# Softmax sums from a column of ones, weights turned first, and gates taken by ScalarE, in a two-part transformer kernel

## The chip, the cores and the metric

The kernel runs on one core of a Trainium2 chip. Time is device time in microseconds (us) of one launch of the whole program. An engine's instructions run in the order in which they were issued to it; the engines run beside each other and wait for each other through semaphores. TensorE (PE) multiplies matrices and turns tiles, VectorE (DVE), ScalarE (ACT) and GpSimd (POOL) work element by element, SyncE (SP) issues the transfers (DMAs). TensorE writes to PSUM alone[...]; GpSimd does not touch it.

## The reference, cut to what matters

The input has 8 sequences of 512 tokens and 128 channels, in float32. A first part normalises it and adds an attention of 16 heads with another weighting than the softmax; the change does not touch it. The second part runs six layers, each an attention over a window and a gated feed-forward:

```python
def local_attention(q, k, v):            # 16 heads of 64, windows of 32 tokens
    ...
    bk2, bv2 = (look(bk), look(bv))      # each window with the one before it: 64 keys
    ...
    sim = jnp.einsum('bhwie,bhwje->bhwij', bq, bk2) * QK_SCALE
    sim = jnp.where(mask, -jnp.finfo(sim.dtype).max, sim)
    attn = jax.nn.softmax(sim, -1)
    out = jnp.einsum('bhwij,bhwje->bhwie', attn, bv2)

def ffn_layer(x, g, bln, W1, b1, W2, b2):
    ...
    hg = xn @ W1 + b1
    a, gate = jnp.split(hg, 2, -1)       # 341 columns each
    return a * jax.nn.gelu(gate, approximate=False) @ W2 + b2

for i in range(DEPTH):                   # 6
    x = attn_layer(shift_tokens(x), Wqkv[i], q_scale[i], k_scale[i], Wo[i]) + x
    x = ffn_layer(shift_tokens(x), ln_g[i], ln_b[i], W1[i], b1[i], W2[i], b2[i]) + x
```

Ahead of the scores q and k are divided by their norms, scaled and rotated.

## The kernel before

The second part goes through layers, in a layer through the 8 sequences, in a sequence through two halves of 8 heads: 96 halves. A half is four pairs of heads, so there are 384 pairs, and the loop at the end takes one step t for each. A pair passes through several steps, so that one step works on several pairs at once. In a step, in the order of the text:

- `turn` (pair t): TensorE turns q and k, 8 transposes (L619), ScalarE copies them out (L624).
- `share` (pair t-2): VectorE sums the exponentials of a row (L662) and takes the reciprocal (L665) into `rs`, which the next step reads.
- `gather` (pair t-3): TensorE multiplies the turned weights with v, 32 small products of 64 keys by 32 queries by 64 columns, two instructions each (L685); VectorE multiplies what comes out with `rs` (L693).
- `turn_weights` (pair t-2): TensorE turns the exponentials (L673), ScalarE copies them out (L674).
- `prepare_qk`, for a quarter of the tokens of the next half: q and k of 8 heads (L552); ScalarE squares them (L557), VectorE sums the squares (L558) and multiplies with the rotary tables (L560, L568 twice), for q and then for k; GpSimd adds and scales (L572, L580); the norms go over L575 (VectorE), L576 and L577 (ScalarE).
- `exponentials` (pair t-1): ScalarE, L657. The text pins it behind all that stands ahead of it on ScalarE.
- `turn_sums` (pair t-3): TensorE turns the sums (L701), ScalarE copies them (L705).
- `weigh` (pair t): 32 small products for the scores (L639), VectorE adds the mask (L644) and takes the maxima (L649), GpSimd subtracts them (L650).
- `prepare_v`: v for a quarter of the tokens (L588), which ScalarE copies into `v` (L592). After the fourth quarter `spread` issues 18 DMAs on SP's queue (L604 to L609) that lay v out as `v3`, each window's keys on the partitions; `v3` is there twice, `v` once.
- one stage of a feed-forward, if one is under way, and then `leave` (pair t-3): the product with the output's weights (L711).

A feed-forward takes its stages in successive steps and comes once in 8 steps: turn the tokens (L733), normalise (L739 to L746), turn back (L753), the gates (L761 on TensorE; L764, VectorE, adds the bias and brings them from PSUM to `gate`), the other columns (L771, L774), and the product back to 128 channels (L782, L785). The gelu (L722) is done on ScalarE in the step after the gates, with a load of its table ahead of it and of the usual one behind it. By the step number modulo 8, its place, the stages stand so: L733 in place 4, L739 to L746 in 5, L753 in 6, L761 in 7, L771 in 0, L782 in 1; places 2 and 3 have none.

PSUM: five banks go round for the products and transposes of TensorE (tag "mm"), one buffer of two banks (tag "two") serves the scores and the sums of v in turn, one bank is the accumulator. So L685 has to wait until L644 has read the scores of the step before, and L639 until L693 has read the sums.

Order: the text is written through a library whose planner lays down each engine's order. It goes by the order of the text, with times of its own for each instruction, and lets a later instruction pass one whose operands or buffer are, by these times, not there yet. In the trace ScalarE's copies of v (L592) stand up to three steps behind their place in the text, and VectorE's L764 between L644 and L649. In all steps of the second part TensorE's order is that of the text.

Of the kernel before, what the change touches and what calls it, by code (L numbers as in the profile page):

```python
# [9 lines left out]
F32 = mybir.dt.float32  # L10
BF16 = mybir.dt.bfloat16
AF = mybir.ActivationFunctionType
ALU = mybir.AluOpType
AX = mybir.AxisListType
PSUM = bass.MemoryType.PSUM

P = 128
N = 512
NT = N // P
# [10 lines left out]
DHL = 64  # L30
INNER = H * DHL
NPAIR = H // 2
WIN = 32
QB = 32
KB = QB + WIN
NQ = N // QB
UB = P // QB
HH = H // 2
HC = HH * DHL
# [7 lines left out]
NCH = len(CH)  # L47
# [3 lines left out]
def tile_kernel(  # L51
# [18 lines left out]
    nc = tc.nc  # L70
# [38 lines left out]
    with ExitStack() as c1:  # L109
# [69 lines left out]
        xs = []  # L179
# [211 lines left out]
        for w in range(len(work) + 1):  # L391
            before, now, nxt = now, nxt, []
            if w + 1 < len(work):
                b, rbs = work[w + 1]
# [27 lines left out]
    k2 = ctx.enter_context(tc.tile_pool(name="k2", bufs=1))  # L422
    wp = ctx.enter_context(tc.tile_pool(name="wp", bufs=1))
    ep = ctx.enter_context(tc.tile_pool(name="ep", bufs=2))
    qp = ctx.enter_context(tc.tile_pool(name="qp", bufs=2))
    vp = ctx.enter_context(tc.tile_pool(name="vp", bufs=2))
    wo_p = ctx.enter_context(tc.tile_pool(name="wo_p", bufs=1))
    wf = ctx.enter_context(tc.tile_pool(name="wf", bufs=2))
    tp = ctx.enter_context(tc.tile_pool(name="tp", bufs=2))
# [4 lines left out]
    gate = wo_p.tile([P, NCH, N], F32, name="gate")  # L434
# [39 lines left out]
    rows = ep.tile([DEPTH, NV, P], F32, name="rows", tag="v", bufs=1)  # L474
# [8 lines left out]
    vec = k2.tile([P, NV, DEPTH], F32, name="vec")  # L483
# [45 lines left out]
    def shifted(b, name):  # L529
# [5 lines left out]
        nc.gpsimd.tensor_copy(xs[hf:D, 1:N], xT[hf:D, b, 0 : N - 1])  # L535
        return xs

    def begin(l, b, hv, xs):

        qn = [qp.tile([P, NT, HH, DHL], F32, name=f"qn{t}") for t in range(2)]  # L540
        v = ep.tile([P, NT, HC], F32, name="v", bufs=1)
        v3 = vp.tile([P, NQ, HC // 2], F32, name="v3")
        return dict(l=l, b=b, hv=hv, xs=xs, qn=qn, v=v, v3=v3)

    def prepare_qk(g, wqkv, tab, c):

# [35 lines left out]
            )  # L582

    def prepare_v(g, wqkv, c):
        xs, v = g["xs"], g["v"]
        lhsT = xs[:, c * P : (c + 1) * P]
        pv = ps_a.tile([P, HC], F32, name="pv2", tag="mm")
        nc.tensor.matmul(  # L588
            pv, lhsT=lhsT, rhs=wqkv[:, 2, :],
            start=True, stop=True,  # L590
        )
        nc.scalar.copy(v[:, c, :], pv)  # L592

    def spread(g):


        v, v3 = g["v"], g["v3"]
        for e in range(2):
            at = slice(e * KB, e * KB + WIN)
            cols = slice(e * (HC // 2), (e + 1) * (HC // 2))  # L600
            for u in range(UB):
                own = v[u * QB : (u + 1) * QB, :, cols]
                c = 1 if u == 0 else 0
                nc.sync.dma_start(v3[e * KB + WIN : (e + 1) * KB, u + c * UB :: UB, :], own[:, c:])  # L604
                if u < UB - 1:
                    nc.sync.dma_start(v3[at, u + 1 :: UB, :], own)
                else:
                    nc.sync.dma_start(v3[at, UB::UB, :], own[:, 0 : NT - 1])
            nc.sync.dma_start(v3[e * KB : (e + 1) * KB, 0, :], v[0:KB, 0, cols])  # L609


    def turn(a):
# [43 lines left out]

        tc.keep_in_program_order(nc.scalar.activation(flat, flat, AF.Exp))  # L657

    def share(a):

        a["rs"] = rs = tp.tile([P, 2 * NT], F32, name="rs", bufs=3)
        nc.vector.tensor_reduce(  # L662
            rs, a["pr"].rearrange("p c e k -> p (c e) k"), axis=AX.X, op=ALU.add
        )
        nc.vector.reciprocal(rs, rs)  # L665

    def turn_weights(a):

        pr = a["pr"]
        a["prT"] = prT = tp.tile([P, NT, P], F32, name="prT")  # L670
        pT = ps_a.tile([P, NT, P], F32, name="pT2", tag="mm")
        for c in range(NT):
            nc.tensor.transpose(pT[:, c, :], pr[:, c].rearrange("p e k -> p (e k)"), ident)  # L673
        nc.scalar.copy(prT, pT)  # L674

    def gather(a):

        g, p, prT = a["g"], a["p"], a["prT"]
        po = ps_b.tile([P, 2, N], F32, name="po2", tag="two")
        po = po[:, :, 0 : NT * DHL].rearrange("p e (c f) -> p e c f", c=NT)  # L680
        for n in range(NQ):
            c, u = n // UB, n % UB
            for e in range(2):
                rows = slice(e * KB, (e + 1) * KB)
                nc.tensor.matmul(  # L685
                    po[u * QB : (u + 1) * QB, e, c, :],
                    lhsT=prT[rows, c, u * QB : (u + 1) * QB],
                    rhs=g["v3"][rows, n, p * DHL : (p + 1) * DHL],
                    start=True, stop=True,
                )  # L690
        a["o"] = o = tp.tile([P, NT, 2, DHL], F32, name="o2")
        by = a["rs"].rearrange("p (c e) -> p e c", e=2).unsqueeze(3)
        nc.vector.tensor_tensor(  # L693
            o.rearrange("p c e f -> p e c f"), po, by.to_broadcast([P, 2, NT, DHL]), ALU.mult
        )

    def turn_sums(a):
# [28 lines left out]
    def feed_forward(b, l, w1, w2):  # L726

        xs = shifted(b, "xf")
        yield

        px = ps_a.tile([P, NT, D], F32, name="px", tag="mm")
        for c in range(NT):
            nc.tensor.transpose(px[:, c, :], xs[:, c * P : (c + 1) * P], ident)  # L733
        xt = tp.tile([P, NT, D], F32, name="xt", bufs=1)
        nc.scalar.copy(xt, px)
        st = tp.tile([P, NT, 6], F32, name="st")
        mv = tp.tile([P, NT, 2], F32, name="mv")
        for c in range(NT):
            nc.vector.bn_stats(st[:, c, :], xt[:, c, :])  # L739
            nc.vector.bn_aggr(mv[:, c, :], st[:, c, :])  # L740
        yield
        rn = tp.tile([P, NT], F32, name="rn")
        nc.scalar.activation(rn, mv[:, :, 1], AF.Ln, bias=eps_ln)
        nc.scalar.activation(rn, rn, AF.Exp, scale=-0.5)
        for c in range(NT):
            nc.vector.tensor_scalar(  # L746
                xt[:, c, :], xt[:, c, :], mv[:, c, 0:1], rn[:, c : c + 1],
                ALU.subtract, ALU.mult,
            )
        yield  # L750
        pn = ps_a.tile([P, N], F32, name="pn", tag="mm")
        for c in range(NT):
            nc.tensor.transpose(pn[:, c * P : (c + 1) * P], xt[:, c, :], ident)  # L753
        xn = tp.tile([P, N], F32, name="xn_ffn", bufs=1)
        nc.scalar.activation(
            xn, pn, AF.Identity, bias=vec[:, 1, l : l + 1], scale=vec[:, 0, l : l + 1]
        )
        yield
        for k, (c0, cn) in enumerate(CH):
            gp = ps_a.tile([P, N], F32, name="gp", tag="mm")  # L760
            nc.tensor.matmul(  # L761
                gp[:cn], lhsT=w1[:, DI + c0 : DI + c0 + cn], rhs=xn, start=True, stop=True
            )
            nc.vector.tensor_scalar(  # L764
                gate[:cn, k], gp[:cn], vec[:cn, 3 + NCH + k, l : l + 1], None, ALU.add
            )
        waiting.append(gate)
        yield
        for k, (c0, cn) in enumerate(CH):
            ap = ps_a.tile([P, N], F32, name="ap", tag="mm")  # L770
            nc.tensor.matmul(  # L771
                ap[:cn], lhsT=w1[:, c0 : c0 + cn], rhs=xn, start=True, stop=True
            )
            nc.vector.scalar_tensor_tensor(  # L774
                gate[:cn, k], ap[:cn], vec[:cn, 3 + k, l : l + 1], gate[:cn, k],
                ALU.add, ALU.mult,
            )
        tc.no_sync_barrier()
        yield
        y = ps_a.tile([P, N], F32, name="y2", tag="mm")  # L780
        for k, (c0, cn) in enumerate(CH):
            nc.tensor.matmul(  # L782
                y, lhsT=w2[:cn, k, :], rhs=gate[:cn, k], start=(k == 0), stop=(k == NCH - 1)
            )
        nc.vector.scalar_tensor_tensor(  # L785
            xT[:, b, :], y, vec[:, 2, l : l + 1], xT[:, b, :], ALU.add, ALU.add
        )
        if l == DEPTH - 1:
            xr = tp.tile([P, NT, D], F32, name="xr")
            nc.sync.dma_start(xr, x2[b].rearrange("(c p) d -> p c d", p=P))  # L790
            yield
            pf = ps_a.tile([P, NT, D], F32, name="pf", tag="mm")
            for c in range(NT):
                nc.tensor.transpose(pf[:, c, :], xT[:, b, c * P : (c + 1) * P], ident)
            nc.vector.tensor_tensor(xr, xr, pf, ALU.add)
            nc.sync.dma_start(out[b].rearrange("(c p) d -> p c d", p=P), xr)
# [35 lines left out]
    while t < len(halves) * PH + LAG + 1 or parts:  # L832
        i, p = t // PH, t % PH
        a = done = last = ahead = None
        if 0 <= i < len(halves):
            a = dict(g=groups[i], p=p)
            pairs.append(a)
        if LAG <= t < len(pairs) + LAG:
            done = pairs[t - LAG]
# [2 lines left out]
        if a:  # L842
            turn(a)
        if done:
            share(done)
        if last:
            gather(last)
        if done:
            turn_weights(done)

        i, c = (t + 1) // PH + 1, (t + 1) % PH
        if i < len(halves):
# [16 lines left out]
        if last:  # L869
            l, b, hv = (last["g"][n] for n in ("l", "b", "hv"))  # L870
# [61 lines left out]
```

## Time and profile before

| | us |
|---|---|
| median of 3 runs | 5099.17 (5098.44 to 5099.74) |
| the profiled execution | 5096.4 |
| its span, first to last instruction | 5094.7 |
| second part, from about | 1668 |
| a step of the second part, mean | 8.8 |
| TensorE busy in the span | 4212.5 |
| VectorE | 4292.8 |
| ScalarE | 3544.0 |
| GpSimd | 2982.7 |

How to read it: the busy times overlap, since the engines run beside each other. A row of a group gives the line in the code, the engine, what it writes and reads, the shapes, the count, then the busy time in all, the mean of one in nanoseconds, and how long the engine had stood idle ahead of it and for whom. A row of the timeline gives the start, the length, and the instruction; in brackets stands how long the engine waited and what ended the wait. A row of the waits gives who waited for whom, the sum, the number of times and the longest. A row by stretch gives the stretch, its length, then busy time and instructions of TensorE, its weight loads, VectorE, ScalarE and GpSimd, the granted clock of TensorE, the share of DMA and GB/s. TensorE's ends are modelled.

### The profile page before, as it was taken

Reading aid. Unit: us, or ns where it says so; the run is one execution under the profiler, and the core shown is the slowest. Engines: PE = TensorE matmul, PEld = TensorE weight load, DVE = VectorE, ACT = ScalarE, POOL = GpSimd, SP = SyncE. Lnnn points to the kernel's source line nnn. Section 1 sums busy time; section 2 is a strip of 40 time slices with the busy share of each in tenths; the row PEclk is TensorE's granted clock in tenths of the full one; section 3 lists DMA queues with packets and bytes.
Section 4 is the critical chain, followed back from the end, with each engine's and each line's share of the span. In section 5 each row is a group of like instructions: output and inputs, shape, how many; then the busy total and the mean of one; then the engine's idle time right before and its main releaser. Section 6 shows DMA issues by size and latency. Waiting matters only on the chain.

```text
span 5094.7 us, 163374 instructions
## 1 busy us (share of the span) xinstructions
PE 4212.5 (83%) x67981; PEld 2491.9 (49%) x67981; DVE 4292.8 (84%) x11404; ACT 3544.0 (70%) x6314; POOL 2982.7 (59%) x3827
## 2 busy tenths in 40 slices
PE   4556566556554899999999999999999999999998
PEld 1223233223322555555555555565555555556555
DVE  7789888888887888888888888888888888888886
ACT  6889999999898566665666666656666566665664
POOL 2444434444445766666666666666666666666663
PEclk7667667667665999999999999999999999999999
DMA  0000000000001323232233222332223223233231
GB/s 9 1 5 1 5 5 1 5 3 3 3 1 26 72 58 73 61 76 64 56 73 72 65 67 58 74 75 56 69 58 81 68 55 72 61 76 73 62 75 47
DMA packets 273626, 237.61 MB, mean 47 GB/s; under 512 B 47056, under 2 KB 269048, under 8 KB 272888
## 3 DMA queue, kind: packets, MB, share of 16 engines
q1 hardware_dynamic: 272888, 227.16, 19.0%
q8 instruction: 538, 8.81, 0.8%
q14 instruction: 200, 1.64, 0.1%
HBM read 21.52 MB, written 4.19 MB: 5 GB/s over the span
## 4 chain that ended last, share of the span: by engine, by line
PE 43%; DVE 30%; ACT 19%; POOL 5%; issue 2%; SPq 0%; DMA 0%; ACTq 0%; POOLq 0%; DVEq 0%
PE m L552 9%; PE po L685 6%; DVE qr L568 5%; DVE stw L300 5%; DVE ss L558 5%; ACT d L297 5%; DVE qn L560 5%; PE pT L673 4%; PE acc L711 3%; ACT d L298 3%; PE ptq L619 3%; PE pv L588 3%; POOL da L263 2%; PE y L782 2%; PE gp L761 2%
## 5 line engine op out<-in xcount | busy, mean ns | idle before, releaser
L572 POOL TENSOR_TENSOR qn<-qn,qr 128x512 f32<-128x512 f32 x768 | 977.8, 1273 | 1047.4 <-DVE qr L568 827.2
L580 POOL TENSOR_TENSOR qn<-qn,ss 128x512 f32<-128x512 f32 x768 | 784.7, 1043 | 58.6 <-ACT ss L577 58.6
L558 DVE TENSOR_REDUCE ss<-sq 128x8 f32<-128x512 f32 x768 | 521.4, 679 | 351.0 <-ACT sq L557 351.0
L263 POOL TENSOR_TENSOR df<-ns,lam 128x32 f32<-128x32 f32 (+7 forms) x1024 | 396.9, 425 | 604.9 <-DVE lam L315 390.7
L552 PE MATMUL m<-wqkv,xs 128*128 128x512 f32 x1536 | 726.9, 596 | 2.0 <-ACT v L592 1.7
L297 ACT ACTIVATE d<-ns,lam 128x416 f32<-128x416 f32 (+7 forms) x1024 | 559.5, 615 | 64.9 <-DVE stw L300 27.5
L557 ACT ACTIVATE sq<-m 128x512 f32<-128x512 f32 x768 | 453.8, 597 | 187.4 <-PE m L552 184.7
L568 DVE TENSOR_TENSOR qr<-m,tab 128x256 f32<-128x256 f32 x1536 | 570.6, 412 | 0.0
L300 DVE BATCH_NORM_STATS2 stw<-d 128x6 f32<-128x416 f32 (+7 forms) x1024 | 514.6, 561 | 56.1 <-ACT d L298 55.7
L248 PE MATMUL s<-kn,qj 32*32 32x160 f32 (+15 forms) x4096 | 423.6, 491 | 151.4 <-DVE mn L253 136.6
L624 ACT COPY qT<-ptq 128x512 f32<-128x512 f32 x768 | 419.9, 579 | 175.1 <-PE ptq L619 175.1
L338 PE MATMUL dTp<-ident,da 128*128 128x128 f32 x1280 | 295.3, 371 | 294.8 <-issue 68.6
L560 DVE TENSOR_TENSOR qn<-m,tab 128x512 f32<-128x512 f32 x768 | 521.5, 679 | 0.0
L263 POOL TENSOR_TENSOR da<-ns,lam 128x416 f32<-128x416 f32 (+15 forms) x512 | 310.7, 639 | 319.3 <-PE dTp L338 252.5
L619 PEld LDWEIGHTS ptq<-ident,qn 128*128 128x128 f32 x3072 | 360.0, 141 | 210.4 <-issue 157.6
L685 PE MATMUL po<-v,prT 64*32 64x64 f32 x24576 | 389.3, 223 | 87.0 <-DVE pr L644 86.9
L588 PE MATMUL pv<-wqkv,xs 128*128 128x512 f32 x768 | 431.8, 644 | 4.9
L650 POOL TENSOR_TENSOR pr<-pr,nm 128x512 f32<-128x512 f32 x384 | 400.8, 1044 | 19.3 <-PE ptq L619 8.8
L711 PE MATMUL acc<-oT,wo 128*128 128x512 f32 x768 | 397.6, 599 | 14.9 <-ACT oT L705 14.9
L619 PE MATMUL ptq<-ident,qn 128*128 128x128 f32 x3072 | 399.3, 273 | 7.2 <-DVE qr L568 3.6
L338 PEld LDWEIGHTS dTp<-ident,da 128*128 128x128 f32 x1280 | 198.5, 186 | 422.3 <-issue 208.7
L685 PEld LDWEIGHTS po<-v,prT 64*32 64x32 f32 x24576 | 323.5, 105 | 166.5 <-DVE pr L644 136.5
(139 smaller groups left out, 8477.1 us busy)
## 6 DMA issues: line engine op xcount, KB each, us to landing
v<-v SPq DMA_DIRECT2D x1152, 128.0 KB
v<-v SPq DMA_DIRECT2D x384, 96.0 KB
v<-v SPq DMA_DIRECT2D x192, 64.0 KB
wqkv<-in_L_ffn_Wqkv_dram SPq DMA_DIRECT2D x24, 256.0 KB
wqkv<-in_L_ffn_Wqkv_dram SPq DMA_DIRECT2D x24, 128.0 KB
wo<-in_L_ffn_Wo_dram SPq DMA_DIRECT2D x12, 256.0 KB
xb<-in_L_attn_x_dram SPq DMA_DIRECT2D x8, 256.0 KB
x<-xb SPq DMA_DIRECT2D x8, 256.0 KB
```

The lines of the kernel that those rows point to most:

```text
L263: nc.gpsimd.tensor_tensor(o, n, by.to_broadcast([P, keys(W, a)]), ALU.add)
L297: nc.scalar.activation(dv[a], nv[a], AF.Ln, bias=lam[:, c : c + 1])
L300: nc.vector.bn_stats(st[:, 4 * j + a].rearrange("p u k -> p (u k)"), dv[a])
L552: nc.tensor.matmul(m.rearrange("p h e -> p (h e)"), lhsT=lhsT, rhs=wqkv[:, t, :], start=True, stop=True,)
L558: nc.vector.tensor_reduce(ss[:, t, :], sq, axis=AX.X, op=ALU.add)
L560: nc.vector.tensor_tensor(qc, m, tab[:, 2 * t, c, :].unsqueeze(1).to_broadcast([P, HH, DHL]), ALU.mult)
L568: nc.vector.tensor_tensor(qr[:, :, u, :], mh[:, :, 1 - u, :], sw.unsqueeze(1).to_broadcast([P, HH, hd]), ALU.mult,)
L572: nc.gpsimd.tensor_tensor(qc, qc, qr.rearrange("p h u e -> p h (u e)"), ALU.add)
L580: nc.gpsimd.tensor_tensor(qc, qc, ss[:, t, :].unsqueeze(2).to_broadcast([P, HH, DHL]), ALU.mult)
L588: nc.tensor.matmul(pv, lhsT=lhsT, rhs=wqkv[:, 2, :], start=True, stop=True,)
L619: nc.tensor.transpose(pt[:, c * P : (c + 1) * P], g["qn"][t][:, c, 2 * p : 2 * p + 2, :].rearrange("p h e -> p (h e)"), ident,)
L685: nc.tensor.matmul(po[u * QB : (u + 1) * QB, e, c, :], lhsT=prT[rows, c, u * QB : (u + 1) * QB], rhs=g["v3"][rows, n, p * DHL : (p + 1) * ...
```

## The change

`share` goes. `v` gets a 65th column of ones for each head, set once, and is one lasting tile; `v3` is laid out likewise, so each row that a DMA moves has 4 x 65 = 260 elements for 256. L685 then yields 65 columns, the last of which is the sum of the weights, and VectorE takes the reciprocal of that from PSUM ahead of L693. `turn_weights` stands ahead of `gather`. The gates are brought out of PSUM by ScalarE, with their bias.

```diff
@@ -535,12 +535,15 @@
         nc.gpsimd.tensor_copy(xs[hf:D, 1:N], xT[hf:D, b, 0 : N - 1])
         return xs
 
+
+    v = k2.tile([P, NT, 2, NPAIR // 2, DHL + 1], F32, name="v")
+    nc.gpsimd.memset(v.rearrange("p c e h d -> p (c e h) d")[:, :, DHL:], 1.0)
+
     def begin(l, b, hv, xs):
 
         qn = [qp.tile([P, NT, HH, DHL], F32, name=f"qn{t}") for t in range(2)]
-        v = ep.tile([P, NT, HC], F32, name="v", bufs=1)
-        v3 = vp.tile([P, NQ, HC // 2], F32, name="v3")
-        return dict(l=l, b=b, hv=hv, xs=xs, qn=qn, v=v, v3=v3)
+        v3 = vp.tile([P, NQ, NPAIR // 2, DHL + 1], F32, name="v3")
+        return dict(l=l, b=b, hv=hv, xs=xs, qn=qn, v3=v3)
 
     def prepare_qk(g, wqkv, tab, c):
 
@@ -582,31 +585,34 @@
             )
 
     def prepare_v(g, wqkv, c):
-        xs, v = g["xs"], g["v"]
+        xs = g["xs"]
         lhsT = xs[:, c * P : (c + 1) * P]
         pv = ps_a.tile([P, HC], F32, name="pv2", tag="mm")
         nc.tensor.matmul(
             pv, lhsT=lhsT, rhs=wqkv[:, 2, :],
             start=True, stop=True,
         )
-        nc.scalar.copy(v[:, c, :], pv)
+        nc.scalar.copy(
+            v[:, c, :, :, 0:DHL],
+            pv.rearrange("p (e h d) -> p e h d", e=2, d=DHL),
+        )
 
     def spread(g):
 
 
-        v, v3 = g["v"], g["v3"]
+        v3 = g["v3"].rearrange("p n h d -> p n (h d)")
+        vc = v.rearrange("p c e h d -> p c e (h d)")
         for e in range(2):
             at = slice(e * KB, e * KB + WIN)
-            cols = slice(e * (HC // 2), (e + 1) * (HC // 2))
             for u in range(UB):
-                own = v[u * QB : (u + 1) * QB, :, cols]
+                own = vc[u * QB : (u + 1) * QB, :, e]
                 c = 1 if u == 0 else 0
                 nc.sync.dma_start(v3[e * KB + WIN : (e + 1) * KB, u + c * UB :: UB, :], own[:, c:])
                 if u < UB - 1:
                     nc.sync.dma_start(v3[at, u + 1 :: UB, :], own)
                 else:
                     nc.sync.dma_start(v3[at, UB::UB, :], own[:, 0 : NT - 1])
-            nc.sync.dma_start(v3[e * KB : (e + 1) * KB, 0, :], v[0:KB, 0, cols])
+            nc.sync.dma_start(v3[e * KB : (e + 1) * KB, 0, :], vc[0:KB, 0, e])
 
 
     def turn(a):
@@ -656,14 +662,6 @@
 
         tc.keep_in_program_order(nc.scalar.activation(flat, flat, AF.Exp))
 
-    def share(a):
-
-        a["rs"] = rs = tp.tile([P, 2 * NT], F32, name="rs", bufs=3)
-        nc.vector.tensor_reduce(
-            rs, a["pr"].rearrange("p c e k -> p (c e) k"), axis=AX.X, op=ALU.add
-        )
-        nc.vector.reciprocal(rs, rs)
-
     def turn_weights(a):
 
         pr = a["pr"]
@@ -677,7 +675,7 @@
 
         g, p, prT = a["g"], a["p"], a["prT"]
         po = ps_b.tile([P, 2, N], F32, name="po2", tag="two")
-        po = po[:, :, 0 : NT * DHL].rearrange("p e (c f) -> p e c f", c=NT)
+        po = po[:, :, 0 : NT * (DHL + 1)].rearrange("p e (c f) -> p e c f", c=NT)
         for n in range(NQ):
             c, u = n // UB, n % UB
             for e in range(2):
@@ -685,13 +683,15 @@
                 nc.tensor.matmul(
                     po[u * QB : (u + 1) * QB, e, c, :],
                     lhsT=prT[rows, c, u * QB : (u + 1) * QB],
-                    rhs=g["v3"][rows, n, p * DHL : (p + 1) * DHL],
+                    rhs=g["v3"][rows, n, p, :],
                     start=True, stop=True,
                 )
         a["o"] = o = tp.tile([P, NT, 2, DHL], F32, name="o2")
-        by = a["rs"].rearrange("p (c e) -> p e c", e=2).unsqueeze(3)
+        rs = tp.tile([P, 2, NT], F32, name="rs")
+        nc.vector.reciprocal(rs, po[:, :, :, DHL])
         nc.vector.tensor_tensor(
-            o.rearrange("p c e f -> p e c f"), po, by.to_broadcast([P, 2, NT, DHL]), ALU.mult
+            o.rearrange("p c e f -> p e c f"), po[:, :, :, 0:DHL],
+            rs.unsqueeze(3).to_broadcast([P, 2, NT, DHL]), ALU.mult,
         )
 
     def turn_sums(a):
@@ -761,8 +761,8 @@
             nc.tensor.matmul(
                 gp[:cn], lhsT=w1[:, DI + c0 : DI + c0 + cn], rhs=xn, start=True, stop=True
             )
-            nc.vector.tensor_scalar(
-                gate[:cn, k], gp[:cn], vec[:cn, 3 + NCH + k, l : l + 1], None, ALU.add
+            nc.scalar.activation(
+                gate[:cn, k], gp[:cn], AF.Identity, bias=vec[:cn, 3 + NCH + k, l : l + 1]
             )
         waiting.append(gate)
         yield
@@ -842,11 +842,9 @@
         if a:
             turn(a)
         if done:
-            share(done)
+            turn_weights(done)
         if last:
             gather(last)
-        if done:
-            turn_weights(done)
 
         i, c = (t + 1) // PH + 1, (t + 1) % PH
         if i < len(halves):
```

## The prediction

> **What bounds the kernel now.** I read the page first, then the busy time by stretch, the waits of the second part, and the timelines of single steps.
>
> ```profile
> PE 4212.5 (83%) x67981; PEld 2491.9 (49%) x67981; DVE 4292.8 (84%) x11404; ACT 3544.0 (70%) x6314; POOL 2982.7 (59%) x3827
> 3000.00:4000.00 1000.00, 957.89 (x17615) 590.60 (x17616) 857.44 (x1879) 608.86 (x1236) 666.55 (x653) 1.00 0.29 68
> DVE ss L558 <- ACT sq L557: 207.4, 196, 1.4
> PEld po L685 <- DVE pr L644: 80.2, 142, 1.5
> PE po L685 <- DVE pr L644: 50.9, 80, 1.2
> ```
>
> The averages of the page mix two parts; the change touches the second alone (from about 1668 us, 384 steps of 8.8 us). There TensorE is busy 96% at full clock, VectorE 86%, ScalarE 61%. VectorE is not the bound by its sum: it stands idle each step until the squares arrive. What TensorE waits for on the path is L685, the sums of v, for the bank that L644 empties.
>
> The steps repeat every 8. Averaged over places 0 to 7 (step number modulo 8), counted from the first transpose of L619: TensorE is through with L619 at 0.97 us in all. The bank is free (L644's end) before 0 in places 0 to 2, and at 1.24, 1.29, 0.86, 2.19, 0.86 us in places 3 to 7. The exponentials that L673 turns (L657's end) are there before 0 in the first two, mostly in place 2, but at 1.96, 2.06, 1.29, 2.95, 1.29 us in places 3 to 7. Place 4, from the timelines:
>
> ```profile
> 2983.68 1.04 PE L619 MATMUL ptq<-ident,qn 128*128 128x128 f32 x8
> 2985.04 0.86 PE L685 MATMUL po<-v,prT 64*32 64x64 f32 x64 [0.32 <-DVE pr L644]
> 2985.83 0.66 PE L673 MATMUL pT<-ident,pr 128*128 128x128 f32 x4
> ...
> 2984.43 0.22 ACT L576 ACTIVATE ss<-ss 128x16 f32<-128x16 f32 x1 [2.61 <-DVE ss L575]
> 2984.55 0.57 ACT L624 COPY qT<-ptq 128x512 f32<-128x512 f32 x1
> 2985.01 0.22 ACT L577 ACTIVATE ss<-ss 128x16 f32<-128x16 f32 x1
> 2985.13 0.62 ACT L657 ACTIVATE pr<-pr 128x512 f32<-128x512 f32 x1
> ```
>
> L657 ends at 2985.75, L673 starts at 2985.83. So today the sums of v cover the wait for the exponentials: the step that the change moves forward is the one whose input comes last.
>
> **Weights turned first.** If TensorE gets L673 ahead of L685 everywhere, L673 starts at exp + 0.08, L685 0.49 us after it (the time from L673 to L552 today), and L552 0.79 after that (1.44 in places 3 and 7, where L685 is long). Today L552 starts after: 3.24, 2.63, 2.25, 3.53, 2.85 us in places 3 to 7. In the new order: 2.04+0.49+1.44 = 3.97 (+0.73), 2.14+1.28 = 3.42 (+0.79), 1.37+1.28 = 2.65 (+0.40), 3.03+1.28 = 4.31 (+0.78), 1.37+0.49+1.44 = 3.30 (+0.45). Behind L673 would stand L685, then both products of L552, and all of VectorE's next chain (L558 to L644) waits for those: the delay passes to the next step in full. In places 0 to 2 the exponentials are early and the order costs and gains nothing.
>
> Here a rule speaks against the change. The Trainium skill, "TensorE: Matmul & The Clock Gate", section "Part 2: What happens when you issue a matmul", says that only weight loads are pulled ahead; matmuls stay in order. So the chip will not pass a waiting L673, and the issued order decides. The trace agrees as far as it goes: with 1.21 us idle ahead of L685 in place 6 no product slips in. But the issued order is the planner's, not the text's: it lets a later instruction pass one whose operands it takes to be missing. It does so on TensorE too; L350 is written as one block, and yet:
>
> ```profile
> 1665.80 0.41 PE L350 MATMUL po<-dT,va 128*32 128x128 f32 x2
> 1666.21 0.49 PE L379 MATMUL pr<-wT,oT 128*128 128x128 f32 x2
> 1666.63 0.64 PE L350 MATMUL po<-dT,va 128*32 128x128 f32 x14
> ```
>
> In places 3, 4 and 6 the planner put one qT copy between L576 and L577, so in its reckoning too L619's first half is done just then, and L577 and L657 (0.22 + 0.62) are still to come when L619's second half ends. L673 is not ready there, L685 nearly is. I take it that L685 stays first in these three. By the rule with the written order the sum would be +2.3 us a cycle (below); by the planner's order, 0. In places 5 and 7 L657 is planned ahead of both copies and it is open: 0 or +0.40 and +0.45. Place 5's delay would be absorbed, since place 6 waits for a VectorE stretch that begins ahead of it; place 7's would not: 0 to 0.45 x 48 = 0 to 22 us. I take 0.
>
> **Column of ones.** Gone: L662 and L665. Added: a reciprocal out of PSUM ahead of L693.
>
> ```profile
> L662 DVE TENSOR_REDUCE rs<-pr 128x8 f32<-128x512 f32 x227 | 152.5, 672 | 2.1
> L665 DVE RECIPROCAL rs<-rs 128x8 f32<-128x8 f32 x227 | 45.0, 198 | 4.8
> 1668.41 0.26 DVE L368 RECIPROCAL den<-pq 128x16 f32<-128x16 f32 x1 [0.38 <-PE pq L366]
> ```
>
> VectorE saves 0.67 + 0.20 - 0.26 = 0.61 us a step, 234 us in all, but nearly everywhere in its idle time ahead of L558 (0.75 to 1.39 us). It is worth something where VectorE sets the step. Place 5 is that one:
>
> ```profile
> 2993.99 0.65 DVE L662 TENSOR_REDUCE rs<-pr 128x8 f32<-128x512 f32 x1
> 2994.56 0.17 DVE L740 BATCH_NORM_AGGREGATE mv<-st 128x2 f32<-128x6 f32 x1
> ...
> 2995.67 1.10 DVE L746 TENSOR_SCALAR xt<-xt,mv,rn 128x128 f32<-128x128 f32 x3 [0.26 <-ACT rn L744]
> 2996.70 0.67 DVE L558 TENSOR_REDUCE ss<-sq 128x8 f32<-128x512 f32 x1
> ```
>
> Without L662 the last L740 comes 0.57 us sooner, so do L743, L744, L746 and L558, and place 6's L685 waits that much less. The squares, held on ScalarE behind L743, move too. From 0.3 to 0.57; I take 0.5: 48 x 0.5 = **24 us off**.
>
> The new reciprocal puts L693's end some 0.2 us later after L685: about 1.0 us. L701 needs it; between lie the products of L552, 1.72 us. Covered by 0.7 us; without that cover 0.26 x 384 = 100 us. L685 has 65 columns for 64: between nothing (64 issues in 0.79 us are 12 ns each[...]) and 1/64 of 0.79 us x 384 = 5 us. I take **4 us on**.
>
> **v and its DMAs.** The copy L592 writes the same 512 elements per partition (0.59 us). Rows go from 1024 to 1040 bytes, 18 DMAs per half as before. In the trace a 1024-byte packet took 71 ns (median), a 2048-byte one 84, so about 71 here. The Trainium skill, "DMA: Bandwidth & Descriptors", section "How a descriptor splits into AXI transactions", says that a run off a 256-byte boundary also pays the bytes below its start: at most 40 beats for 32, an estimate of 89 ns, or 180 packets per us on 16 engines where some 200 are seen. The half that starts at 3002.13 then has its last packet at 3020.4 instead of 3019.1; the next L592 starts at 3022.74. Nothing by either. SP's queue has no other work in that stretch; the memset of ones is one small instruction on POOL.
>
> **Gates.** 144 of L764 (739 ns) leave VectorE, and 144 activations with a bias come to ScalarE; nearest is L755, 784 ns, also Identity out of PSUM: 113 us. It is place 7, and ScalarE is idle from 3013.60 to 3016.21 and from 3017.18 to 3018.71 around that. The next exponentials may come up to 0.8 us later, but have 1.8 us to spare in place 0. Nothing either way; at worst 0.7 x 48 = 36 us if a gate holds up a qT copy.
>
> **Sum.** The profiled execution: 5094.7 span + 1.7 around it = 5096.4. Less 24, plus 4: 5076. The median of the runs is 2.8 above the profiled one: **5079 us**.
>
> **Rivals.**
> 1. L673 goes first in place 7 (and 5) too. For: L657 is planned ahead of both copies there, and ScalarE's and TensorE's ends lie within 0.3 us. 5079 + 22 = 5101, no change.
> 2. Slower: L673 goes first in all steps, as written. The place is the end of L619, the price the wait for L657. +0.73 +0.79 +0.32 (place 6, its 0.78 less VectorE's 0.5) +0.45 = 2.3 us x 48 = 110, with the columns 5213. It decides once places 3 and 4 are turned (1.5 us against the 0.5 gained). Against: the planner's habit above.
> 3. Packets of 1040 bytes are cut in two: 18 issues of 1.2 us for 0.6, landing near 3030, ScalarE held up to 7 us at L592 in every second half: 48 x 7 = 336, some 5430. Against: rows of 2728 bytes went as single packets.
> 4. The planner rearranges copies of v, oT or gates otherwise: plus or minus 25 us.
>
> **Chances.** Forecast 0.45; rival 1, 0.25; rival 2, 0.12; rival 3, 0.03; rival 4, 0.15, two thirds of it slower. Within 0.2% (5089 to 5109, about what these runs can tell from no change) lie most of rival 1 (0.20), the upper tail of the forecast (0.03) and a little of rival 4 (0.03): same 0.26. Faster: the rest of the forecast and 0.02 of rival 4: 0.44. Slower: rivals 2 and 3, 0.05 of rival 1, 0.10 of rival 4: 0.30. The range leaves out rivals 2 and 3 and a tail of 0.04: 5055 to 5140. The forecast's own is 5064 to 5089.
>
> **What would show it.** Right: L685 ahead of L673 in places 3, 4 and 6; L685's wait in place 6 down from 1.2 to about 0.7 us; VectorE near 79% busy in the second part; L701 starting at once after L552; places 0 to 2 unchanged. Wrong: a wait "pT L673 <- ACT pr L657" on TensorE of 0.4 us or more, a wait of L701 for L693, or L592 waiting for a DMA.

## The result and the profile after

The changed kernel takes 5213.19 us (median; 5209.61 to 5214.3), the kernel before, measured beside it, 5099.45: 1.022 times as long, 95% interval 1.021 to 1.0234. The forecast was 5079. The profiled execution has a span of 5210.5 us, against 5094.7.

The engines' busy times and one stretch of the second part, from the page and from the busy times by stretch:

```profile
PE 4273.6 (82%) x67981; PEld 2481.2 (48%) x67981; DVE 4012.6 (77%) x10876; ACT 3626.2 (70%) x6458; POOL 2983.3 (57%) x3828
...
3000.00:4000.00 1000.00, 947.46 (x17084) 570.35 (x17083) 752.88 (x1676) 611.66 (x1240) 645.54 (x635) 1.00 0.29 65
```

VectorE's busy time fell by 280 us, and it is busy 75% there instead of 86%. TensorE is busy 94.7% of that millisecond for 95.8%, but gets through 17084 products for 17615. So the time was lost on TensorE.

The edit moves the lines: the sums of v are now L683 (L685 before), the turned weights L671 (L673), the exponentials L663 (L657), q and k L555 (L552). In the experiments they move again by a few; the names of the tiles stay (po<-v, pT, pr, m).

The waits of the second part (3000 to 5000 us: sum, times, longest):

```profile
DVE rs L691 <- PE po L683: 333.0, 190, 3.1
PEld pT L671 <- ACT pr L663: 50.6, 111, 0.6
PEld po L683 <- DVE pr L650: 50.0, 79, 0.8
PE po L683 <- DVE pr L650: 31.3, 79, 0.6
PE pT L671 <- ACT pr L663: 25.0, 84, 0.3
```

The wait for the scores' bank is smaller than before (31.3 for 50.9 us, weight loads 50.0 for 80.2). New is the wait of the turned weights (L671) for the exponentials (L663). VectorE's new wait for the sums (L691) lies in its idle time. Place 4, TensorE's and ScalarE's timelines:

```profile
3027.54 1.04 PE L625 MATMUL ptq<-ident,qn 128*128 128x128 f32 x8
3028.90 0.46 PE L683 MATMUL po<-v,prT 64*32 64x65 f32 x32 [0.33 <-DVE pr L650]
3029.66 0.65 PE L671 MATMUL pT<-ident,pr 128*128 128x128 f32 x4 [0.30 <-ACT pr L663]
3030.25 0.46 PE L683 MATMUL po<-v,prT 64*32 64x65 f32 x32
3030.64 1.98 PE L555 MATMUL m<-wqkv,xs 128*128 128x512 f32 x4
...
3028.99 0.62 ACT L663 ACTIVATE pr<-pr 128x512 f32<-128x512 f32 x1
```

The sums of v are cut in two. Half of them run, then the transposes stand and wait for L663, which ends at 3029.61, and the other half waits behind them. The planner did this in place 3 (32 and 32 instructions, in 40 of 45 steps counted), in place 4 (32 and 32, in all) and in place 6 (50 and 14, in all). In places 5, 7, 0, 1 and 2 the transposes come first as a whole.

A cycle is eight steps, one of each place. The steps' mean lengths by place, from the starts of the q and k transposes in the traces (us; 45 cycles each):

| place | before | after | order alone | order undone | ones alone | exponentials early | both |
|---|---|---|---|---|---|---|---|
| 0 | 11.05 | 11.11 | 11.10 | 11.06 | 11.06 | 11.62 | 11.62 |
| 1 | 9.81 | 9.81 | 9.82 | 9.77 | 9.77 | 9.73 | 9.73 |
| 2 | 7.16 | 7.28 | 7.25 | 7.17 | 7.16 | 7.27 | 7.27 |
| 3 | 8.12 | 8.27 | 8.28 | 8.13 | 8.13 | 7.67 | 7.69 |
| 4 | 7.93 | 8.49 | 8.48 | 7.93 | 7.94 | 7.67 | 7.67 |
| 5 | 7.34 | 8.54 | 7.69 | 7.55 | 7.55 | 8.47 | 7.68 |
| 6 | 8.83 | 8.76 | 9.18 | 8.63 | 8.63 | 7.90 | 7.87 |
| 7 | 10.29 | 10.46 | 10.47 | 10.32 | 10.32 | 9.86 | 9.84 |
| sum | 70.53 | 72.72 | 72.28 | 70.56 | 70.55 | 70.20 | 69.38 |

The other columns are the runs below. The cycle is 2.19 us longer, 105 us over 48 cycles, of the 116 between the spans; the rest lies ahead of the first step (3 us) and in the first and last steps. The 2.19 come in three pieces. Ahead of the first product of q and k (L555) it is 0.72: 0.46 and 0.48 more in places 4 and 5, less 0.22 in the other six. Behind it each place but 5 takes 0.06 to 0.17 more, 0.74 in all. Place 5 alone takes 0.73 more there, because the turned sums (L701) come late:

```profile
3038.76 1.98 PE L555 MATMUL m<-wqkv,xs 128*128 128x512 f32 x4
3041.41 0.63 PE L701 MATMUL po<-ident,o 128*128 128x128 f32 x4 [0.67 <-ACT sq L560]
...
3039.59 0.20 DVE L691 RECIPROCAL rs<-po 128x8 f32<-128x8 f32 x1
3039.71 0.96 DVE L746 TENSOR_SCALAR xt<-xt,mv,rn 128x128 f32<-128x128 f32 x1
3040.59 0.68 DVE L692 TENSOR_TENSOR o<-po,rs 128x512 f32<-128x512 f32 x1
...
3039.54 1.04 POOL L656 TENSOR_TENSOR pr<-pr,nm 128x512 f32<-128x512 f32 x1
```

The division (L692) ends at 3041.27 and L701 starts 0.14 later. The bracket names the squares (L560), which were done at 3041.38, but it is the division that L701 waits for: in all 45 cycles of this place it starts 0.15 us after the division's end, and it does so too in the run with the order undone (below), where the squares end 0.38 us after L701 has begun. Between reciprocal and division the planner put a normalisation of the feed-forward (L746), and it takes 0.96 us beside GpSimd's L656.

### The profile page after: what moved, and what is told of

Read it like the earlier page. It is cut to its first block, busy times and chain, and to the rows that moved or that the text cites. A ratio compares the mean times of both kernels' runs of the same rounds, so it can differ in the third digit from the quotient of the medians.

```text
span 5210.5 us, 163206 instructions
## 1 busy us (share of the span) xinstructions
PE 4273.6 (82%) x67981; PEld 2481.2 (48%) x67981; DVE 4012.6 (77%) x10876; ACT 3626.2 (70%) x6458; POOL 2983.3 (57%) x3828
## 4 chain that ended last, share of the span: by engine, by line
PE 43%; DVE 25%; ACT 24%; POOL 5%; issue 3%; DMA 0%; SPq 0%; ACTq 0%; POOLq 0%; DVEq 0%
PE m L555 11%; PE po L683 6%; DVE qr L571 5%; DVE ss L561 5%; DVE stw L300 5%; ACT d L297 4%; DVE qn L563 4%; PE pT L671 4%; PE acc L711 3%; ACT d L298 3%; PE pv L591 3%; ACT sq L560 3%; PE ptq L625 3%; POOL da L263 2%; PE y L782 2%
## 5 line engine op out<-in xcount | busy, mean ns | idle before, releaser
L583 POOL TENSOR_TENSOR qn<-qn,ss 128x512 f32<-128x512 f32 x768 | 785.6, 1044 | 58.4 <-ACT ss L580 58.4
L560 ACT ACTIVATE sq<-m 128x512 f32<-128x512 f32 x768 | 459.4, 598 | 485.7 <-PE m L555 483.0
L555 PE MATMUL m<-wqkv,xs 128*128 128x512 f32 x1536 | 764.8, 620 | 2.0 <-ACT v L595 1.7
L561 DVE TENSOR_REDUCE ss<-sq 128x8 f32<-128x512 f32 x768 | 522.0, 680 | 238.1 <-ACT sq L560 238.1
L691 DVE RECIPROCAL rs<-po 128x8 f32<-128x8 f32 x384 | 79.0, 206 | 581.9 <-PE po L683 581.9
L683 PE MATMUL po<-v,prT 64*32 64x65 f32 x24576 | 387.2, 224 | 56.8 <-DVE pr L650 56.7
L656 POOL TENSOR_TENSOR pr<-pr,nm 128x512 f32<-128x512 f32 x384 | 400.5, 1043 | 23.3 <-DVE nm L655 21.8
```

The lines of the kernel that those rows point to most:

```text
L555: nc.tensor.matmul(m.rearrange("p h e -> p (h e)"), lhsT=lhsT, rhs=wqkv[:, t, :], start=True, stop=True,)
L560: nc.scalar.activation(sq, m, AF.Square)
L561: nc.vector.tensor_reduce(ss[:, t, :], sq, axis=AX.X, op=ALU.add)
L583: nc.gpsimd.tensor_tensor(qc, qc, ss[:, t, :].unsqueeze(2).to_broadcast([P, HH, DHL]), ALU.mult)
L683: nc.tensor.matmul(po[u * QB : (u + 1) * QB, e, c, :], lhsT=prT[rows, c, u * QB : (u + 1) * QB], rhs=g["v3"][rows, n, p, :], start=True, s ...
```

## The experiments

Theory A: the order costs the time, since the turned weights' input is late. Theory B: the column of ones does, through the reciprocal between sums and division. Theory C: the gates on ScalarE do. A fourth was added after the first runs, theory D: the new sequence of small and full products costs it, whether its input is early or late.

**Order undone.** The changed kernel with the old order:

```diff
+        if last:
+            gather(last)
         if done:
             turn_weights(done)
-        if last:
-            gather(last)
```

> The changed kernel with the sums of v ahead of the turned weights again; the column of ones and the gates on ScalarE stay. Theory A, the order costs the time (the turned weights stand on TensorE ahead of the sums of v while their exponentials are still to come): the steps of places 3, 4, 5 and 7 win back 0.05, 0.46, 0.48 and 0.07 us, and the product after the sums of v the 0.05 us it lost in each of 8 places, 1.46 us x 48 = 70: about 5143, and between 5090 and 5145. Theory B, the column of ones costs it (the reciprocal stands between the sums of v and what turns them): 5190 or more. Theory C, the gates on ScalarE cost it: 5190 or more.

Measured: 5106.66 us, 1.0014 times the kernel before (1.0007 to 1.0021). One edit takes back 106 of the 114 us, somewhat more than theory A gave it. B and C, which had the loss stay, fall as its main cause.

**Order alone.** The kernel before with the two calls swapped:

```diff
         if done:
             share(done)
+            turn_weights(done)
         if last:
             gather(last)
-        if done:
-            turn_weights(done)
```

> The kernel before with the turned weights ahead of the sums of v and nothing else. Theory A: some 70 us more than before, 5150 to 5200. Theories B and C: as before, 5085 to 5115.

Measured: 5188.68 us, 1.0174 (1.0159 to 1.0189), 90 us more. Its timeline of place 4 shows the same cut and the same wait, with 64 columns:

```profile
3091.88 0.46 PE L685 MATMUL po<-v,prT 64*32 64x64 f32 x32 [0.32 <-DVE pr L644]
3092.64 0.66 PE L673 MATMUL pT<-ident,pr 128*128 128x128 f32 x4 [0.31 <-ACT pr L657]
3093.23 0.45 PE L685 MATMUL po<-v,prT 64*32 64x64 f32 x32
```

The two runs do not add up: 90 for the order, and 7 for the rest, leave 17 of the 114 for the two together. By the table they lie in place 5: 8.54 us together, where the order alone has 7.69, the rest alone 7.55 and the kernel before 7.34; place 6 gives 0.22 of that back.

**Ones alone and gates alone.** The kernel before with the column of ones (order and gates as before), and with the gates' edit only:

> The kernel before with the column of ones alone; order and gates as before. Theory A: 5075 to 5100 (24 us off for the sums that VectorE no longer makes, if nothing of its own is added). Theory B: 5150 to 5215. Theory C: as theory A.

> The kernel before with the gates taken out of PSUM by ScalarE, and nothing else. Theories A and B: 5090 to 5110. Theory C: 5130 or more.

Measured: 5102.69 (1.0008, 0.9999 to 1.0016) and 5102.62 (1.0009, 1.0 to 1.0017). Neither gain nor loss can be told from nothing here, and the ones do not bring the 24 us that the prediction gave them; their run lies just above theory A's stretch. With the ones place 6 is 0.20 us shorter and place 5 0.21 longer. VectorE's timeline of place 5 in that run:

```profile
3070.19 0.17 DVE L691 RECIPROCAL rs<-po 128x8 f32<-128x8 f32 x1
3070.88 0.45 DVE L746 TENSOR_SCALAR xt<-xt,mv,rn 128x128 f32<-128x128 f32 x1 [0.51 <-ACT rn L744]
3071.25 0.68 DVE L692 TENSOR_TENSOR o<-po,rs 128x512 f32<-128x512 f32 x1
3071.85 0.99 DVE L746 TENSOR_SCALAR xt<-xt,mv,rn 128x128 f32<-128x128 f32 x3
```

The sums of a row are gone, but the division stands behind a normalisation that itself waits 0.51 us for ScalarE, and all four normalisations now come ahead of L561, where before the fourth came later.

**Ones alone, normalisations behind the division.** The same with the four of them issued behind that step's division:

> The column of ones alone (5103 in its own run), with the normalisations held behind the division. If the ones' gain of 0.2 us in place 6 was given back in place 5 by a normalisation between reciprocal and division: place 5 back to 7.34 us and 10 to 25 us below the kernel before, 5074 to 5090. If the ones had no gain to give: 5095 to 5110.

Measured: 5103.26 (1.0005, 0.9997 to 1.0014). The gain that was hoped for did not come. Place 5 fell to 7.12 us, but place 6 rose to 9.07: together 16.19, for 16.18 with the ones alone and 16.17 before. Issued behind the division, the four normalisations hold up L561 instead:

```profile
3062.68 0.69 DVE L692 TENSOR_TENSOR o<-po,rs 128x512 f32<-128x512 f32 x1
3063.28 1.83 DVE L747 TENSOR_SCALAR xt<-xt,mv,rn 128x128 f32<-128x128 f32 x4
3065.04 0.67 DVE L561 TENSOR_REDUCE ss<-sq 128x8 f32<-128x512 f32 x1
```

So in these two runs, in the old order, the ones give nothing by themselves: what one of the two places gains on VectorE the other loses.

**Exponentials early.** If the late input is the cause, bringing it early must turn the loss. In the changed kernel `prepare_qk` is split ahead of the norms (L578 to L583, now `norms`), and the exponentials are called between the two:

```diff
-            prepare_qk(ahead, wq[ahead["hv"]], tab[ahead["l"]], c)
+            ss = prepare_qk(ahead, wq[ahead["hv"]], tab[ahead["l"]], c)
         if 1 <= t < len(pairs) + (0 if a else 1):
             exponentials(pairs[t - 1])
+        if ahead:
+            norms(ahead, ss, c)
```

> The changed kernel with each pair's exponentials put one place earlier on ScalarE: behind the squares, ahead of the two norm activations, so that they no longer wait for VectorE's chain. Nothing is left out. Theory A, the late exponentials are what the new order pays for: the wait of the turned weights for them goes, the sums of v wait for their bank alone, and the first product of places 3 to 7 starts 0.45, 0.90, 0.54, 0.93 and 0.07 us earlier in its step, 2.9 us x 48 = 139: about 5074, between 5055 and 5110. Theory D, the new sequence itself costs it (products of small tiles next to full ones, sums of v cut in two): 5190 or more.

Measured: 5093.59 (0.999, 0.9983 to 0.9997), 120 us off the changed kernel. Theory D falls as the main cause; a part of it stays, named below under "The sum of rival 2". The blocks are whole again in all eight places. Place 4 with the weights turned first and no wait, TensorE's timeline:

```profile
3052.62 1.04 PE L628 MATMUL ptq<-ident,qn 128*128 128x128 f32 x8
3053.50 0.60 PE L674 MATMUL pT<-ident,pr 128*128 128x128 f32 x4
3054.03 0.86 PE L686 MATMUL po<-v,prT 64*32 64x65 f32 x64
3054.82 1.99 PE L555 MATMUL m<-wqkv,xs 128*128 128x512 f32 x4
```

Here the first products start 2.20 us after the step does, for 3.09, as expected to 0.01; over a cycle they come 3.6 us sooner, for the 2.9 expected. Yet some 20 us of the expected gain are missing. Place 0 lost 0.5 us, where the exponentials now stand between the gelu's second table load and the copy of the turned sums on ScalarE. In place 5 the division's delay grew: L701's counterpart now starts 3.11 us after the first product, for 2.65, since the products come 0.54 us sooner in the step and the division only 0.07.

**The same in the old order.**

> The kernel before with the exponentials put ahead of the two norm activations, and nothing else. Theory A: there the sums of v cover the wait already (weights turned at 2.14 us, exponentials there at 2.06), so nothing is gained: 5085 to 5110. If it is as fast as the changed kernel with early exponentials, the new order is worth nothing even where its input is there.

Measured: 5089.07 (0.9983, 0.9976 to 0.9991). Early exponentials are worth 120 us in the new order and 9 in the old one. So it is in the main their lateness that the new order pays for. Two limits: the edit also puts the norms later, which was not tried apart; and in this run's trace the planner does not keep the old order everywhere. In place 3 (40 of 45 steps), 4 and 6 it puts two of the four transposes ahead of the sums of v, so some of the 9 us may come from that.

**Normalisations behind the division, in the changed kernel, and both.** The edit of the run with the ones, in the changed kernel:

```diff
-        for c in range(NT):
-            nc.vector.tensor_scalar(
+        with tc.issue_after(latest["o"].ins):
+            for c in range(NT):
+                nc.vector.tensor_scalar(
```

`latest["o"]` is the division that `gather` issued last.

> The changed kernel with the four normalisations of place 5 held behind that step's division of the sums on VectorE, so that none stands between the reciprocal and the division. Theory A with this as its second part: place 5's turned sums start 0.8 us sooner behind the products, but the normalisations come later and place 6 gives about half of it back, as in the run of the order alone: 5185 to 5200. If the delay there is no fault of them: 5205 to 5220.

> Both: exponentials early and normalisations behind the division. Theory A: some 20 us below the run with early exponentials alone, about 5055, between 5035 and 5085. Theory D: 5170 or more.

Measured: 5183.38 (1.0165, 1.015 to 1.0181), 30 us off and a little more than expected, with the turned sums of place 5 at 1.82 us after the first product again, for 2.65; and **5049.13 with both (0.9903, 0.9888 to 0.9917)**, faster than either kernel. VectorE in place 5 of the run of both:

```profile
3043.61 0.17 DVE L694 RECIPROCAL rs<-po 128x8 f32<-128x8 f32 x1
3043.82 0.69 DVE L695 TENSOR_TENSOR o<-po,rs 128x512 f32<-128x512 f32 x1
3044.43 1.57 DVE L750 TENSOR_SCALAR xt<-xt,mv,rn 128x128 f32<-128x128 f32 x3
3045.93 0.67 DVE L561 TENSOR_REDUCE ss<-sq 128x8 f32<-128x512 f32 x1
```

**What the order is worth then, and place 0.** The run of both with the old order, and with the exponentials also ahead of the gelu in place 0 (the call of `gelus()` moved from the end of `prepare_qk` to behind `exponentials`):

> The run of both (5049) with the sums of v ahead of the turned weights again. What the new order is worth once its input is early. Theory A: the sums of v again put 0.49 us into the loop from the bank's release to the products in places 3, 4, 6 and 7 and win 0.05 in each place by the cheaper sequence: 4 x 0.4 less 8 x 0.05 = 1.2 us, x 48 = 55: about 5100, between 5070 and 5110. If the order is worth nothing even then: 5040 to 5060.

> As the run of both (exponentials early, normalisations behind the division), but in place 0 the exponentials also stand ahead of the gelu and its two table loads. Theory A: place 0, 9.43 us from the first product to the next step where it was 8.91, gets its 0.5 us back, x 48 = 25: about 5025, between 5010 and 5040. If there they wait for GpSimd's subtraction and hold the gelu up by as much: 5045 or more.

Measured: 5093.76 (0.9991, 0.9984 to 0.9998): the new order in the text is worth 45 us once its input is early. Here too the planner put two of the four transposes first in places 3, 4 and 6, so the 45 us are the gain over its order and not over the old one as written. And 5048.95 (0.9899, 0.9882 to 0.9915): nothing more than with both. Place 0 stays at 11.62 us; the gelu starts later by what the exponentials no longer take behind it. That expectation failed, its alternative held.

## Why the prediction was wrong

- **What bounds the kernel**: right. TensorE's wait at the sums of v, and VectorE's chain from L558 to the bank's release, set the step; 0.61 us a step off VectorE did nothing by itself.
- **Weights turned first**: this is the step that failed, "I take it that L685 stays first in these three" and "I take 0" for places 5 and 7. The reasoning weighed two whole blocks. But L685 is 64 instructions, and the planner changed over within them, after half in places 3 and 4 and after 50 in place 6. These are the steps in which the prediction had seen a qT copy between L576 and L577 (place 3 in 40 of 45 here too), so its sign told where the planner does not follow the text, but not that it would cut a block. That it changes over once it takes the exponentials to be there is inferred: with early ones every block is whole. In places 5 and 7 it turned the weights first (rival 1). Even so the first products came only 0.05 us later in place 3 and 0.07 in place 7; the loss ahead of them sits in places 4 (+0.46, for +0.79 in the written order) and 5 (+0.48, for +0.40). Place 5's delay was not absorbed by place 6, whose products started 0.18 us earlier in their step, not the 0.5 that had been counted on. No run put the whole block of transposes first while the exponentials were late, so what the cut itself costs or saves is open.
- **The sum of rival 2**, 5213, was met to the microsecond by luck, since its terms were not. It had the waits ahead of the products in places 3, 4, 6 and 7, 2.3 us a cycle. These four come to 0.40, and all eight to 0.72. The rest is two terms that the working lacked. One: the turned sums come 1.82 us after the first product, for 1.72, when the small products of L683 stand directly ahead of L555; it is there in every place of the runs in the new order and not in the old one, with 64 columns as with 65. Ahead of the products, in the places without a wait, the new order wins back 0.06. Two: place 5's division, 0.73, which takes the order and the ones together: with the order alone that place has no such delay.
- **Column of ones**: "24 us off" failed too; nothing came. The row was right, place 6's wait did shrink (0.20 us with the ones alone, 0.3 expected at the least and 0.5 taken), and place 5 gave it back, through a normalisation that slipped in where the new reciprocal makes the division wait. "Covered by 0.7 us" held in seven places and not in place 5. There a normalisation stood ahead of the division, and with the ones alone the turned sums came 2.13 us after the first product for 1.72. The 65th column cost nothing (4 taken): with the ones alone the products start at 2.25 us as before in the places without a wait. The reciprocal took 206 ns, for 260.
- **v and its DMAs**: right, nothing waits for them. A packet took 79 ns (median), between the 71 taken from the row and the 89 of the estimate.
- **Gates**: right, no gain and no loss that the runs can tell; 678 ns each for 784.
- **Its own signs**: of the signs of being wrong, the wait of the turned weights for the exponentials came (0.3 us at the longest on the products, 0.6 on the weight loads, for the 0.4 named), and so did L701's wait for the division. VectorE came to 75%, not 79%.
- **Two sums that slipped**, neither with weight: 0.7 x 48 is 34, not 36, and rival 3's 336 us on the forecast make 5415, not 5430.

## What to carry to other kernels

Before a step is moved forward in an in-order queue, look at which of the two neighbours gets its input last, and move the producer first: the same swap cost 90 us alone and 106 in the changed kernel with late exponentials, and won 45 with early ones. Where a planner lays down the order, it may cut a block of many instructions, as it did here after 32 and after 50 of 64, so a forecast has to ask for each instruction, not for each block. And an experiment that puts an order back has to be read in its trace too: in two runs here the planner did not put it back everywhere. Work taken off an engine with idle time was worth nothing by its sum here, and a new dependent pair on that engine, reciprocal and division, opened a gap which the planner filled with work that was not on the path.

## What the runs showed of the hardware that was not expected

A normalisation on VectorE (L746, from SBUF to SBUF, 128x128) took 334 ns on average in 100 of 192 cases of the changed kernel, where GpSimd did nothing beside it, and 692 in the 92 where GpSimd was at work; the one between reciprocal and division took 934 on average, and in the stretch above it ended 0.09 us after GpSimd's L656 (3040.67 and 3040.58). The Trainium skill, "SBUF — State Buffer", section "Who interferes with whom", says that `tensor_scalar` can run, when its operands allow, in a mode that takes the port pair which VectorE shares with GpSimd, and that the later of the two then waits for the whole instruction of the other; the rows fit that. No run here takes GpSimd's work away alone, so the port itself is argued, not shown. Nor did a run find out why full products cost 0.10 us more directly behind small ones; that it goes with the order and not with the columns is shown.
